# Softmax maxima of every logits block reduced to 32 columns of a table in SBUF, instead of one running maximum in PSUM

## The chip, the cores and the metric

The kernel runs on one core of a Trainium2 chip. The metric is the time on the device of one execution, in microseconds (us); less is better. A core has five engines that run side by side and meet only through semaphores: PE multiplies matrices and writes PSUM, DVE does elementwise work and reductions, ACT evaluates functions and copies, POOL does slower elementwise work on SBUF alone, and SP issues transfers. Each engine runs its own instructions in order.

## The reference

Four cross-attention layers run one after the other on a state of 4 batches x 512 positions x 256 channels, against a context of 4 x 1024 keys x 512 channels. Layers 0, 2 and 3 have 16 heads of width 64 and a bias on at most four keys ("masked" layers below); layer 1 has 16 heads of width 16 with 4 shared key/value heads and an RMS norm ahead of it ("grouped").

```python
q = (x @ Wq) split in heads;  k = (ctx @ Wk);  v = (ctx @ Wv)
logits = einsum('bhqd,bhkd->bhqk', q, k) * scale      # 512 queries x 1024 keys per head
logits += col_bias                                    # layers 0, 2, 3: four key columns
probs = softmax(logits, axis=-1)
x = einsum('bhqk,bhkd->bhqd', probs, v) @ Wo + bo + x # layer 1: without bo
```

The change is in the maximum over the keys that the softmax subtracts.

## The kernel before

A **group** is two heads of one batch in one layer. It has 128 groups: 96 masked and 32 grouped. The logits of a group are laid out with keys on the partitions: block t (of `NT` = 8) holds 128 keys on the partitions and 2 heads x 512 queries = 1024 columns, and lies in `g.st[t]` in SBUF. The maximum that a query needs therefore runs over 8 blocks and over the 128 partitions.

**Order.** Two hand-written strings, `MASKED_TURNS` and `GROUPED_TURNS`, lay the groups out in 96 steps. Each step has one masked group `g`; in 32 of them (steps 12 to 19, 22 to 29, 32 to 39 and 68 to 75) a grouped group `lam`, whose logits were made at the end of the step before, is finished beside it. Below these are the *mixed* steps. All instructions are issued in an order written by hand; the order in the source is the order on each engine's queue. One step does, in this order:

1. POOL: `subtract(lam, t)` (L886), the grouped logits less their maximum, 8 times.
2. `scores(g)` (L803 to L817): for each block, PE makes the logits in two banks of PSUM (L803; for block 0 also the bias, L809), ACT copies them to `g.st[t]` (L813), and from block 1 on DVE does `top = max(top, g.st[t])` (L817), where `top` is the first block's own place in PSUM, `g.mx_place`.
3. `max_quarters(g)` on DVE: `over_quarter` (L854) turns each 32 x 32 square of `top` and reduces it, so that 128 x 1024 becomes 128 x 32 in PSUM; then a fold over the four quarters of the partitions: a copy (L864), a maximum (L865), a copy (L866) and four maxima into `g.every` (L869). In every one of these, one input lies in PSUM. `max_everywhere(g)` (L880) turns the 32 columns back into a 128 x 1024 tile: in PSUM for a masked group, in SBUF for a grouped one.
4. `attend(g1)` on PE (L833): the group of the step before times its values.
5. `subtract(g, t)` on DVE (L888), `exponentials(g, t)` on ACT (L894) and, behind each, the running sum of the exponentials on POOL (L933). Behind them `normalise(g1)` on DVE, whose `reciprocal_sums` uses `over_quarter` again (L854 to L968) and `scale_out` (L979).
6. Meanwhile PE fills its time with projections (L514, L553, L608, L721, L997). In a mixed step, `attend(lam)` comes among them (L833), then `keep_even` (L843) and `keep_odd` (L847).
7. If the next step is mixed, `logits_pair(coming, i)` (L780 to L792) four times: PE makes two blocks, ACT copies them (L786), DVE takes the running maximum (L792); behind the last, `max_quarters` and `max_everywhere` of `coming`.

In 40 of the steps without a grouped group (41 to 64 and 77 to 92), keys or values are made by seven products in place of eight; those have small additions on POOL (L580, L591, L645).

**PSUM** has 8 banks. `Place()` takes two neighbouring banks, the pair that was given back longest ago, and `back()` returns them; all of this is settled when the program is written, and the waits follow from who used the banks last. `g.mx_place` is held from a group's first block until L854 has read it; `max_quarters` holds a further single bank while it folds.

Of the kernel before, what the change touches and what calls it, by code (L numbers as in the profile page):

```python
# [12 lines left out]
ALU = mybir.AluOpType  # L13
AX = mybir.AxisListType
PSUM = bass.MemoryType.PSUM

P = 128
B, S, C = 4, 512, 256
T, CT = 1024, 512
NI = S // P  # L20
NT = T // P
# [59 lines left out]
def kernel(ctx: ExitStack, tc: tile.TileContext, a: dict, out: bass.AP):  # L81
    nc = tc.nc
# [8 lines left out]
    def t_(shape, tag, name, bufs=1, dtype=FP):  # L91
        return sb.tile(shape, dtype, tag=tag, name=name, bufs=bufs)
# [35 lines left out]
    def take_set(g):  # L128
        g.set = sets_free.pop(sets_free.index(min(sets_free)))
        g.st = [st_slot((NT + 1) * g.set + t) for t in range(NT)]  # L130
        g.mx = st_slot((NT + 1) * g.set + NT)
# [643 lines left out]
    def logits_pair(g, i):  # L775
        ws = [Place(), Place()]
        for odd in range(2):
            for j in range(2):
                rows = slice(64 * odd + 32 * j, 64 * odd + 32 * (j + 1))
                nc.tensor.matmul(  # L780
                    ws[odd].ap[:, j * S : (j + 1) * S], lhsT=g.kt[rows, i * P : (i + 1) * P],
                    rhs=g.qt[rows, :], start=True, stop=True,
                )
        for odd, w in enumerate(ws):
            t = 2 * i + odd
            nc.scalar.copy(g.st[t], w.ap)  # L786
            if t == 0:
                g.mx_place = w
            else:
                w.back()  # L790
                top = g.mx_place.ap
                nc.vector.tensor_tensor(top, top, g.st[t], ALU.max)  # L792

    def scores(g):
        take_set(g)
        g.mx_place = Place()
        for t in range(NT):

            w = Place() if t else g.mx_place
            m = w.ap  # L800
            keys = slice(t * P, (t + 1) * P)
            for j in range(2):
                nc.tensor.matmul(  # L803
                    m[:, j * S : (j + 1) * S], lhsT=g.kt[g.rows[j], keys], rhs=g.qt[g.rows[j], :],
                    start=True, stop=t > 0,
                )
            if t == 0:
                for j in range(2):
                    nc.tensor.matmul(  # L809
                        m[:, j * S : (j + 1) * S], lhsT=aug_k[g.l][g.rows[j], keys],  # L810
                        rhs=aug_q[g.rows[j], :], start=False, stop=True,
                    )
            nc.scalar.copy(g.st[t], m)  # L813
            if t:
                w.back()
                top = g.mx_place.ap
                nc.vector.tensor_tensor(top, top, g.st[t], ALU.max)  # L817

    def place_out(g, width=1):
        g.place = Place(width)  # L820
# [29 lines left out]

    def over_quarter(out_, of, op):
        nc.vector.tensor_reduce(  # L854
            out_, of.rearrange("p (b x) -> p b x", x=32), AX.X, op, apply_transpose=True
        )

    def max_quarters(g):
        w = Place(1)
        quarter, half = w.ap[:, 0:32], w.ap[0:64, 32:64]  # L860
        other = t_([64, 32], "other_max", f"other_max_{g.name}")
        over_quarter(quarter, g.mx_place.ap, ALU.max)
        g.mx_place.back()
        nc.vector.tensor_copy(other, quarter[64:128, :])  # L864
        nc.vector.tensor_tensor(half, quarter[0:64, :], other, ALU.max)  # L865
        nc.vector.tensor_copy(other[0:32, :], half[32:64, :])  # L866
        g.every = t_([P, 2 * S // 32, 1], "every", f"every_{g.name}")
        for h in range(4):
            nc.vector.tensor_tensor(  # L869
                g.every[32 * h : 32 * (h + 1), :, 0], half[0:32, :], other[0:32, :], ALU.max  # L870
            )
        w.back()

    def max_everywhere(g):
        if g.masked:
# [76 lines left out]
    def reciprocal_sums(g, m):  # L952

        quarter, half = m[:, 0:32], m[0:64, 32:64]
        other = t_([64, 32], "other", f"other_{g.name}")
        short = t_([P, S // 32, 1], "short", f"short_{g.name}")
        over_quarter(quarter, g.acc, ALU.add)
        nc.vector.tensor_copy(other, quarter[64:128, :])
        nc.vector.tensor_tensor(half, quarter[0:64, :], other, ALU.add)
        nc.vector.tensor_copy(other[0:32, :], half[32:64, :])  # L960
        for h in range(4):
            cols = slice(h // 2 * S // 32, (h // 2 + 1) * S // 32)
            nc.vector.tensor_tensor(
                short[32 * h : 32 * (h + 1), :, 0], half[0:32, cols], other[0:32, cols], ALU.add
            )
        nc.vector.reciprocal(short, short)
        g.ot = t_([P, S], "ot", f"ot_{g.name}", bufs=3)
        nc.vector.transpose(  # L968
            g.ot.rearrange("p (c r) -> p c r", r=32), short.to_broadcast([P, S // 32, 32])
        )  # L970

    def normalise(g):
        w = Place(1)
        reciprocal_sums(g, w.ap)
        w.back()
        scale_out(g)
# [80 lines left out]
    def at(n):  # L1057
        return steps[n] if 0 <= n < len(steps) else (None, None)
# [80 lines left out]
    for n in range(len(steps) + 2):  # L1139
        g, lam = at(n)  # L1140
# [77 lines left out]
        def pair(i):  # L1218
            if i == 0:
                behind_exponentials()  # L1220
                take_set(coming)
            logits_pair(coming, i)
            if i == NT // 2 - 1:
                max_quarters(coming)
                max_everywhere(coming)
# [11 lines left out]
        if g:  # L1237
            g.now = NT if masked_at(g.n + 1) else 4
            scores(g)
# [5 lines left out]
        if g:  # L1245
            max_quarters(g)
            max_everywhere(g)
# [144 lines left out]
```

## Time and profile before

| | before |
|---|---|
| median of 3 runs | 3578.74 us (3578.55 to 3579.28) |
| time of the profiled execution | 3578.93 us |
| its span, first to last instruction | 3577.2 us |
| busy: PE / DVE / POOL / ACT | 98% / 85% / 70% / 66% of the span |
| granted PE clock, mean | 0.995 |

The profile is of one execution. Its span leaves out some 1.7 us around the first and the last instruction. "Busy" counts time in which at least one instruction of the engine is under way; matmuls overlap, and their ends are modelled, so a PE that is 98% busy isn't one that works at its peak for 98% of the time. A group of instructions is named by its line in the kernel. In a chain of waits the text names what released each step.

### The profile page before, as it was taken

The page shows a single profiled execution, that of the slowest core. Times are in us where ns is not written, and L with a number is a line of the kernel's source. Part 1 is how long each engine was busy: PE and PEld are TensorE (multiplying, and loading weights), DVE is VectorE, ACT ScalarE, POOL GpSimd, SP SyncE. Part 2 cuts the span into 40 slices and gives each one's busy share as a digit, 9 for nine tenths or more (in the row PEclk, how much of TensorE's full clock was granted, in tenths as well). Part 3 has the DMA queues.
Part 4 walks back from the last instruction along what each step waited for, and adds up shares of the span by engine and source line. Part 5 has one row for each costly group of instructions (what it writes and reads, how often), then busy time and mean ns, then how long its engine had stood idle before and what let it go on. Part 6 is the DMA issues. An engine that isn't in the chain of part 4 may idle for free.

```text
span 3577.2 us, 42743 instructions
## 1 busy us (share of the span) xinstructions
PE 3495.1 (98%) x15390; PEld 1703.6 (48%) x15390; DVE 3045.3 (85%) x4174; ACT 2352.9 (66%) x2737; POOL 2495.9 (70%) x1273
## 2 busy tenths in 40 slices
PE   8999999999999999999999999999999999999998
PEld 4454444444444444444554545454444445454554
DVE  7878788987889978889888888888788988888887
ACT  4565577775777757777565666665577775666664
POOL 3565477774777747777678778777477776769774
PEclk9999999999999999999999999999999999999999
DMA  3222101002100020001001111010201011002110
GB/s 90 62 93 82 56 20 46 23 19 56 39 23 23 19 78 17 23 23 43 27 27 50 33 33 51 27 51 18 57 22 38 23 34 43 26 27 74 33 32 7
DMA packets 159384, 140.16 MB, mean 39 GB/s; under 512 B 42424, under 2 KB 142264, under 8 KB 158660
## 3 DMA queue, kind: packets, MB, share of 16 engines
q1 hardware_dynamic: 153518, 124.32, 11.2%
q0 software_dynamic: 2560, 8.39, 0.7%
q10 hardware_dynamic: 3094, 4.72, 0.6%
q8 instruction: 122, 2.00, 0.2%
q14 instruction: 90, 0.74, 0.1%
HBM read 122.71 MB, written 10.49 MB: 37 GB/s over the span
## 4 chain that ended last, share of the span: by engine, by line
PE 67%; DVE 23%; ACT 7%; issue 3%; POOL 1%; ACTq 0%; DMA 0%; DVEq 0%; SPq 0%; POOLq 0%
PE ps L608 13%; PE ps L803 13%; PE ps L833 13%; PE ps L514 9%; DVE ps L817 8%; PE ps L553 7%; DVE st L888 5%; ACT st L894 4%; PE ps L780 3%; PE ps L721 3%; PE ps L997 3%; DVE ps L854 2%; DVE ps L880 1%; DVE ps L792 1%; ACT st L786 1%
## 5 line engine op out<-in xcount | busy, mean ns | idle before, releaser
L933 POOL TENSOR_TENSOR st<-st 128x1024 f32<-128x1024 f32 x668 | 1581.0, 2367 | 725.6 <-ACT st L894 680.8
L894 ACT ACTIVATE st<-st 128x1024 f32<-128x1024 f32 x1024 | 1036.3, 1058 | 300.1 <-DVE st L888 233.6
L817 DVE TENSOR_TENSOR ps<-ps,st 128x1024 f32<-128x1024 f32 x672 | 828.0, 1232 | 295.7 <-ACT st L813 234.2
L888 DVE TENSOR_TENSOR st<-st,ps 128x1024 f32<-128x1024 f32 x768 | 883.5, 1216 | 3.3
L886 POOL TENSOR_TENSOR st<-st 128x1024 f32<-128x1024 f32 x256 | 596.8, 2374 | 312.4 <-DVE st L880 207.0
L833 PE MATMUL ps<-st,v 128*64 128x512 f32 (+1 forms) x4064 | 800.7, 595 | 9.0 <-ACT st L894 8.9
L813 ACT COPY st<-ps 128x1024 f32<-128x1024 f32 x768 | 716.6, 1048 | 96.5 <-PE ps L809 65.1
L803 PE MATMUL ps<-qt,kt 64*128 64x512 f32 x3072 | 719.5, 601 | 26.4 <-DVE ps L854 19.6
L833 PEld LDWEIGHTS ps<-st,v 128*64 128x64 f32 (+1 forms) x4064 | 241.4, 130 | 550.2 <-issue 435.5
L803 PEld LDWEIGHTS ps<-qt,kt 64*128 64x128 f32 x3072 | 301.9, 186 | 382.4 <-issue 131.3
L514 PE MATMUL ps<-ctx,wk 128*128 128x512 f32 x896 | 417.1, 611 | 2.2 <-ACT ctx L416 1.1
L553 PE MATMUL ps<-wv,ctx 128*128 128x256 f32 x1792 | 408.0, 382 | 0.0
L553 PEld LDWEIGHTS ps<-wv,ctx 128*128 128x128 f32 x1792 | 335.5, 190 | 102.4 <-issue 59.4
L792 DVE TENSOR_TENSOR ps<-ps,st 128x1024 f32<-128x1024 f32 x224 | 276.1, 1232 | 73.3 <-ACT st L786 60.2
L786 ACT COPY st<-ps 128x1024 f32<-128x1024 f32 x256 | 247.4, 1014 | 83.1 <-PE ps L780 80.2
L514 PEld LDWEIGHTS ps<-ctx,wk 128*128 128x128 f32 x896 | 167.3, 193 | 239.5 <-issue 215.5
L608 PE MATMUL ps<-st 128*128 128x128 f32 (+1 forms) x1200 | 229.0, 339 | 6.4 <-ACT ps L631 6.4
L623 ACT COPY st<-ps 128x512 f32<-128x512 f32 x40 | 23.4, 585 | 301.6 <-PE ps L608 301.6
L780 PE MATMUL ps<-qt,kt 32*128 32x512 f32 x1024 | 183.3, 640 | 18.0 <-DVE o L847 9.7
L608 PEld LDWEIGHTS ps<-st 128*128 128x128 f32 x1200 | 158.6, 192 | 75.1 <-issue 65.1
L721 PE MATMUL ps<-x,wq 128*128 128x512 f32 x384 | 186.2, 608 | 1.3 <-ACT x L379 1.1
L997 PE MATMUL ps<-ot,wo 128*128 128x512 f32 x384 | 175.8, 600 | 0.7 <-DVE ot L979 0.7
(177 smaller groups left out, 2833.1 us busy)
## 6 DMA issues: line engine op xcount, KB each, us to landing
ctx<-kept SPq DMA_DIRECT2D x24, 1024.0 KB
wk<-in_L_xattn_Wk_dram SPq DMA_DIRECT2D x47, 512.0 KB
wv<-in_L_xattn_Wv_dram SPq DMA_DIRECT2D x47, 512.0 KB
wq<-in_L_xattn_Wq_dram SPq DMA_DIRECT2D x96, 128.0 KB
wo<-in_L_xattn_Wo_dram SPq DMA_DIRECT2D x96, 128.0 KB
st<-kept SPq DMA_DIRECT2D x4, 2048.0 KB
kept<-st SPq DMA_DIRECT2D x12, 512.0 KB
qt<-qt ACTq DMA_DIRECT2D x32, 128.0 KB
```

What stands on the lines that cost most here:

```text
L514: nc.tensor.matmul(m, lhsT=g.w["k"][:, k, :], rhs=ctx_half[g.b, n][:, k, :], start=(k == 0), stop=(k == KT - 1),)
L553: nc.tensor.matmul(m[:, half * 2 * P : (half + 1) * 2 * P], lhsT=ctx_half[g.b, t // 4][:, k, t % 4 * P : (t % 4 + 1) * P], rhs=g.w["v2"][: ...
L608: nc.tensor.matmul(m if is_keys else m[:, q], lhsT=right[:, k, :] if is_keys else left_[:, k, q], rhs=left_[:, k, :] if is_keys else right ...
L792: nc.vector.tensor_tensor(top, top, g.st[t], ALU.max)
L803: nc.tensor.matmul(m[:, j * S : (j + 1) * S], lhsT=g.kt[g.rows[j], keys], rhs=g.qt[g.rows[j], :], start=True, stop=t > 0,)
L813: nc.scalar.copy(g.st[t], m)
L817: nc.vector.tensor_tensor(top, top, g.st[t], ALU.max)
L833: nc.tensor.matmul(g.po[at, :], lhsT=g.v[:, t, rows], rhs=g.st[t][:, j * S : (j + 1) * S], start=(t == first), stop=(t == last),)
L886: nc.gpsimd.tensor_tensor(g.st[t], g.st[t], g.mb, ALU.subtract)
L888: nc.vector.tensor_tensor(g.st[t], g.st[t], g.mb, ALU.subtract)
L894: nc.scalar.activation(st, st, AF.Exp)
L933: nc.gpsimd.tensor_tensor(g.acc, g.st[0] if t == 1 else g.acc, g.st[t], ALU.add)
```

## The change

The running maximum goes. Every block, the first included, is given to `over_quarter` by itself as soon as it lies in SBUF, and its 128 x 32 result goes to one eighth of a new table `tops` in SBUF (128 x 8 x 32). After the last block one reduction over the eight takes 128 x 256 to 128 x 32, read in strides of 32 elements. The fold over the quarters is as it was, but its operands now lie in `g.every` and in parts of `tops`, so in SBUF. No place in PSUM is held for a maximum, and `scores` and `logits_pair` give each block's place back when ACT has copied it. `reciprocal_sums` takes part of `tops` as its scratch in place of a tile of its own.

```diff
@@ logits_pair
             t = 2 * i + odd
             nc.scalar.copy(g.st[t], w.ap)
-            if t == 0:
-                g.mx_place = w
-            else:
-                w.back()
-                top = g.mx_place.ap
-                nc.vector.tensor_tensor(top, top, g.st[t], ALU.max)
+            w.back()
+            block_max(g, t)
@@ scores
         take_set(g)
-        g.mx_place = Place()
         for t in range(NT):
-            w = Place() if t else g.mx_place
+            w = Place()
...
             nc.scalar.copy(g.st[t], m)
-            if t:
-                w.back()
-                top = g.mx_place.ap
-                nc.vector.tensor_tensor(top, top, g.st[t], ALU.max)
+            w.back()
+            block_max(g, t)
@@
+    tops = t_([P, NT, 32], "tops", "tops")
...
+    def block_max(g, t):
+        over_quarter(tops[:, t, :], g.st[t], ALU.max)
+
     def max_quarters(g):
-        w = Place(1)
-        quarter, half = w.ap[:, 0:32], w.ap[0:64, 32:64]
-        other = t_([64, 32], "other_max", f"other_max_{g.name}")
-        over_quarter(quarter, g.mx_place.ap, ALU.max)
-        g.mx_place.back()
+        g.every = t_([P, 2 * S // 32, 1], "every", f"every_{g.name}")
+        quarter, half, other = g.every[:, :, 0], tops[0:64, 0, :], tops[0:64, 1, :]
+        nc.vector.tensor_reduce(quarter, tops.rearrange("p t b -> p b t"), AX.X, ALU.max)
         nc.vector.tensor_copy(other, quarter[64:128, :])
         nc.vector.tensor_tensor(half, quarter[0:64, :], other, ALU.max)
         nc.vector.tensor_copy(other[0:32, :], half[32:64, :])
-        g.every = t_([P, 2 * S // 32, 1], "every", f"every_{g.name}")
         for h in range(4):
             nc.vector.tensor_tensor(
                 g.every[32 * h : 32 * (h + 1), :, 0], half[0:32, :], other[0:32, :], ALU.max
             )
-        w.back()
@@ reciprocal_sums
         quarter, half = m[:, 0:32], m[0:64, 32:64]
-        other = t_([64, 32], "other", f"other_{g.name}")
+        other = tops[0:64, 1, :]
```

## The prediction

> **What bounds the kernel now.** I read the page's busy times first, then the steps one by one, then waits and timelines of the steps that looked different.
>
> ```profile
> span 3577.2 us, 42743 instructions
> PE 3495.1 (98%) x15390; PEld 1703.6 (48%) x15390; DVE 3045.3 (85%) x4174; ACT 2352.9 (66%) x2737; POOL 2495.9 (70%) x1273
> PE 67%; DVE 23%; ACT 7%; issue 3%; POOL 1%; ACTq 0%; DMA 0%; DVEq 0%; SPq 0%; POOLq 0%
> ```
>
> PE sets the pace, but a quarter of the chain that ended last lies on DVE. The windows by step say where. Below, columns are the window, its length, then busy time of PE, PEld, DVE, ACT, POOL: two mixed steps, then two steps without a grouped group.
>
> ```profile
> 584.50:634.10 49.60, 47.69 (x180) 18.18 (x178) 45.40 (x66) 35.58 (x40) 35.19 (x15) 1.00 0.20 65
> 634.10:675.50 41.40, 40.67 (x204) 20.96 (x202) 36.52 (x46) 33.57 (x38) 35.72 (x17) 1.00 0.09 22
> 1794.80:1826.40 31.60, 31.60 (x108) 12.80 (x106) 28.76 (x40) 19.24 (x23) 24.68 (x15) 1.00 0.08 24
> 1826.40:1855.20 28.80, 28.80 (x186) 18.68 (x184) 25.08 (x35) 18.73 (x23) 18.99 (x13) 1.00 0.10 31
> ```
>
> The last two are PE without a gap: maxima there have room, since a group's blocks are attended only a step later. In the mixed steps DVE is 45.4 of 49.6 and 36.5 of 41.4 us busy, and what is left is mostly the 0.02 to 0.1 us between its instructions. Its timeline in the first of them (start, length, line, idle before):
>
> ```profile
> 588.25 1.25 DVE L880 STREAM_TRANSPOSE st<-every 128x1024 f32<-128x1024 f32 x1
> 589.41 9.23 DVE L817 TENSOR_TENSOR ps<-ps,st 128x1024 f32<-128x1024 f32 x7
> 598.74 1.26 DVE L854 TRANSPOSE_TENSOR_REDUCE ps<-ps 128x32 f32<-128x1024 f32 x1
> 600.04 0.19 DVE L864 COPY other_max<-ps 64x32 f32<-64x32 f32 x1
> 600.27 0.19 DVE L865 TENSOR_TENSOR ps<-ps,other_max 64x32 f32<-64x32 f32 x1
> 600.49 0.18 DVE L866 COPY other_max<-ps 32x32 f32<-32x32 f32 x1
> 600.71 0.76 DVE L869 TENSOR_TENSOR every<-ps,other_max 32x32 f32<-32x32 f32 x4
> 601.58 1.26 DVE L880 STREAM_TRANSPOSE ps<-every 128x1024 f32<-128x1024 f32 x1
> ...
> 618.66 0.69 DVE L847 TENSOR_TENSOR o<-o,ps 64x512 f32<-64x512 f32 x1 [1.18 <-ACT o L843]
> ...
> 628.80 2.57 DVE L792 TENSOR_TENSOR ps<-ps,st 128x1024 f32<-128x1024 f32 x2 [0.41 <-ACT st L786]
> ```
>
> In 50 us DVE waits for others twice, 1.6 us in all; in the next step (1.0, 1.0, 0.5 and 0.6 us) 3.1. So the change is decided in the 32 mixed steps, where DVE has 4.7 us to spare in a pair of 91. POOL at the same time:
>
> ```profile
> 589.63 18.65 POOL L886 TENSOR_TENSOR st<-st 128x1024 f32<-128x1024 f32 x8 [8.84 <-DVE st L880]
> 608.25 17.04 POOL L933 TENSOR_TENSOR st<-st 128x1024 f32<-128x1024 f32 x7
> ```
>
> The reader is to see that the masked group's fold (600.0 to 601.5) falls into POOL's eight subtractions.
>
> **Removed and added on DVE.** Busy time alone: 896 maxima (672 of L817, 224 of L792) x 1.232 = 1104 us and 128 L854 x 1.265 = 162 us go; 1024 reductions of a block from SBUF x 1.257 (the L854 row ps<-st) = 1287 us come, and 128 reductions of 128 x 256. These aren't in the trace; the nearest, L231, takes 0.304 us for 144 columns, L245 0.253 for 96, so 0.0011 a column and 0.42 for 256. A stride of 32 elements costs nothing in the reciprocals (L744 with it 0.254, L966 without 0.253), so 128 x 0.42 = 54 us. Sum +75 us, and that misleads, because the old maxima are a chain. Seven L817 and the L854 take 10.63 us (589.41 to 600.04), 1.34 from start to start for 1.23 of work: each waits for the one before. Blocks in the table don't depend on each other. Independent instructions overlap: L888 starts each 1.13 for 1.22 of work, and L880 of 1.25 at 588.25 is followed by an independent one after 1.16. Bounds for a reduction's start to start: 1.13 to 1.36 (its 1.26 and the 0.10 of a chain). I take 1.16, the other turning instruction: 7 x 1.16 + 1.36 + 0.46 = 9.94, so 0.7 us less per group (0.9 less to 0.7 more), 2.8 us per pair of mixed steps, which has four groups. The fold itself: the operands from SBUF in place of PSUM, some 0.01 each by L854's two rows (1.265 and 1.257): nothing. `other` in the table is written in DVE's own order, behind the fold that read it: nothing. No transfer and no other queue is moved.
>
> [...]
>
> **PSUM.** The place of the maximum is free sooner, and it has been waited for:
>
> ```profile
>   DVE ps L854: 52.4, 32
> ```
>
> These are waits of L803's weight loads and matmuls for L854, 52.4 us in 32 times, all at the start of mixed steps. With a fourth pair of banks PE goes on there, until ACT's copies (1.05 us each) hold it. Where DVE is the limit the gain isn't added to that of DVE; elsewhere it is nothing, as PE has no gap.
>
> **The fold's inputs.** L865 and the four L869 had one input in PSUM and get two in SBUF; the copies L864 and L866 go from SBUF to SBUF. The trace has no such DVE instruction beside a POOL one, apart from the mask's set-up, where POOL issues gathers:
>
> ```profile
> L283 DVE CAST st<-st x3: 426/481/573, 16.2 to 20.9; 128x512 f32<-128x512 bf16 x3
> ...
> L869 DVE TENSOR_TENSOR every<-ps,other_max x512: 177/181/184, 48.8 to 3546.5; 32x32 f32<-32x32 f32 x171
> ```
>
> The same instruction between SBUF and SBUF takes 426 to 573 ns there, while L869, with an input in PSUM, keeps within 177 to 184 over 512 times, whatever POOL does. So I can't take the new fold to be free of POOL. Bounds: at the lower end 0 more, at the upper each of the seven waits for one POOL instruction (L886, 2372 ns): 16.6 us, cut off where POOL runs dry. It does: 608.3 ends the subtractions, and L933 needs exponentials, which need L888, which stands behind the fold. From 600.0 that is 8.2 us, in the next step (fold at 647.2, POOL to 654.3) 7.1; as the fold comes 0.7 sooner, 8 on average. I take the upper end, since the only row of this sort shows a dependence, and seven waits exceed the cap twice over.
>
> [...]
>
> Behind the waiting fold stand L880, eight L888, L1019, the sums (L854 to L979), L847 and the next grouped group's maxima and L880; ACT's exponentials wait for L888 (233.6 us before), POOL's next subtractions for that L880, PE's grouped attend for both. The masked fold meets L886 in 28 of 32 mixed steps; in the first of each run (12, 22, 32, 68) POOL is done or nearly. Grouped folds run before POOL starts. Elsewhere POOL is idle at the fold or has an L591 of 0.7 us, and PE's bound hides it.
>
> **Sum.** 28 x 8 = 224 us of wait. DVE's spare time takes 14 pairs x (4.7 + 2.8) = 105. The last mixed step of each run is followed by one where DVE is 65% busy, which hides about half of 4 x 8: 16. So +103 us: 3578.9 (profiled; the median is 0.2 lower) + 103 = 3682. Own range: 3638 (7 us, the four last folds hidden whole: 196 - 105 - 32 = +59) to 3760 (reductions at 1.36, so 14 x 5.6 more).
>
> **Rivals.**
> A, faster: the fold doesn't wait. For it: 28 folds beside POOL went undisturbed so far; against it: they read PSUM. Then DVE saves 2.8 us in each of 16 pairs, 45 us: 3534; with a good half of L803's 52 us on top 3500, and at 1.36 nothing, 3579.
> B, near even: copies don't meet POOL and the four L869 pass as one, so 1.2 (half an L886) + 2.4 = 3.6 us: 28 x 3.6 = 101 against 105: 3575, 3550 to 3605.
> C, slower on another ground: the reductions do wait for one another (1.36) and the fold doesn't wait: +2.8 us per pair against 4.7 spare; up to 20 us where the spare time lies wrongly: 3590. It decides if the start to start of block reductions is above 1.30.
>
> **How the numbers follow.** Forecast 0.45, A 0.32, B 0.18, C 0.05. 0.2% (7 us) is what a measurement can tell from none. Faster: 0.30 of A and 0.05 of B; same: 0.02 of A, 0.05 of B, 0.01 of C; slower: the rest, 0.57. The predicted time is the likeliest case's, 3682. The range 3520 to 3750 leaves out the low end of A and the high end of the forecast.
>
> **What would show it.** Right: a fold of 7 to 9 us in place of 1.43 in mixed steps, its instructions starting as an L886 ends; mixed pairs of 97 us and more; other steps unchanged; block reductions 1.16 apart; no wait of L803 for a maximum. Wrong: folds of 1.4 us everywhere (A), 3 to 5 us (B), or reductions 1.3 apart (C).

## The result: 5.9% slower, twice the loss that was forecast

| | before | after |
|---|---|---|
| median | 3579.0 us (4 runs, 3578.6 to 3579.9) | 3790.4 us (4 runs, 3789.0 to 3792.8) |
| ratio, 95% interval | | 1.0592 [1.0578, 1.0605] |
| span of the profiled execution | 3577.2 us | 3787.2 us |
| mean granted PE clock | 0.995 | 0.971 |

The change costs 211 us. The forecast was 103, and the time lies above the whole range. First the page of the changed kernel: span, busy times, the shares of the chain that ended last, and two of the costliest groups (line, engine, shapes, count; then busy us and mean ns of one; then idle time before them).

```profile
span 3787.2 us, 42056 instructions
PE 3548.9 (94%) x15390; PEld 1707.9 (45%) x15390; DVE 3332.3 (88%) x4302; ACT 2358.1 (62%) x2737; POOL 2494.0 (66%) x1273
PE 60%; DVE 29%; ACT 8%; issue 2%; ACTq 0%; POOL 0%; DMA 0%; DVEq 0%; POOLq 0%
L848 DVE TRANSPOSE_TENSOR_REDUCE tops<-st 128x32 f32<-128x1024 f32 x1024 | 1175.3, 1209 | 277.7 <-ACT st L807 241.4
L863 DVE TENSOR_TENSOR every<-tops 32x32 f32<-32x32 f32 x512 | 189.5, 370 | 9.7
```

DVE is 287 us busier, and the chain lies less on PE and more on DVE. What DVE waits for POOL lies in this busy time: it shows in the length of the instructions (the idle time before L863 is 9.7 us in all, as it was before L869). So the engines don't meet through semaphores alone, as the section on the chip has it. The block reductions aren't the reason: 1209 ns against 1232 for the old maximum. But L863, four instructions on 32 x 32 elements (L869 before), takes 370 ns each where it took 180. The same two mixed steps as in the prediction, then the two later steps (window, its length, busy time of PE, PEld, DVE, ACT, POOL, then the granted clock):

```profile
594.40:649.50 55.10, 47.90 (x182) 17.50 (x180) 52.51 (x69) 35.40 (x40) 35.18 (x15) 0.94 0.17 58
649.50:697.50 48.00, 43.69 (x206) 21.35 (x204) 45.19 (x47) 33.61 (x38) 35.65 (x17) 0.93 0.07 20
1915.30:1947.00 31.70, 31.70 (x108) 12.85 (x106) 28.31 (x40) 19.42 (x23) 24.80 (x15) 1.00 0.08 25
1947.00:1975.70 28.70, 28.70 (x184) 18.67 (x182) 26.06 (x37) 19.04 (x23) 18.81 (x12) 1.00 0.10 28
```

These two later steps are unchanged (31.6 and 28.8 before). The mixed pair went from 91.0 to 103.1 us, DVE's busy time in it from 81.9 to 97.7, and the granted clock from 1.00 to 0.94 and 0.93. DVE's timeline in the first of the two mixed steps (start, length), and POOL's beside it:

```profile
607.52 0.60 DVE L858 TENSOR_REDUCE every<-tops 128x32 f32<-128x256 f32 x1
608.15 2.20 DVE L859 COPY tops<-every 64x32 f32<-64x32 f32 x1
610.39 2.28 DVE L860 TENSOR_TENSOR tops<-every,tops 64x32 f32<-64x32 f32 x1
612.71 2.26 DVE L861 COPY tops<-tops 32x32 f32<-32x32 f32 x1
615.00 2.87 DVE L863 TENSOR_TENSOR every<-tops 32x32 f32<-32x32 f32 x4
```

```profile
598.62 18.62 POOL L879 TENSOR_TENSOR st<-st 128x1024 f32<-128x1024 f32 x8 [9.17 <-ACT st L807]
623.55 9.72 POOL L926 TENSOR_TENSOR st<-st 128x1024 f32<-128x1024 f32 x4 [6.31 <-ACT st L887]
```

The masked group's fold lasts until POOL's eight subtractions end, at 617.24: three instructions and the first L863 each take about as long as one subtraction (these are 2.33 us apart) in place of 0.18, and the last three L863 pass at once. The table reduction before them, 0.60 us, isn't held. POOL loses nothing: its 256 subtractions are busy for 595.5 us, 596.8 before. What the late fold does to PE shows in PE's timeline (in brackets: idle before, and what ended it):

```profile
614.67 3.60 PE L514 MATMUL ps<-ctx,wk 128*128 128x512 f32 x8
624.01 5.55 PE L825 MATMUL ps<-st,v 128*32 128x512 f32 x28 [5.74 <-ACT qt L727]
```

Between the fold and PE stand these, on DVE and on ACT:

```profile
619.27 3.48 DVE L881 TENSOR_TENSOR st<-st,ps 128x1024 f32<-128x1024 f32 x3
620.52 2.95 ACT L887 ACTIVATE st<-st 128x1024 f32<-128x1024 f32 x3 [9.12 <-DVE st L881]
623.38 0.57 ACT L727 ACTIVATE qt<-ps 128x512 f32<-128x512 f32 x1
```

The reader is to see the chain: the fold, DVE's subtractions L881, ACT's exponentials L887, and behind the first three of them in ACT's queue the evacuation L727 (a copy out of PSUM), at whose end PE finds a place in PSUM. PE waits 5.7 us, and the 28 matmuls behind the wait take 5.55. Before the change the same 28 (L833 there) came without a wait and took 3.63:

```profile
610.20 3.63 PE L833 MATMUL ps<-st,v 128*32 128x512 f32 x28
```

Waits of this sort, the first two rows below, are most of PE's 238 us of idle time in the whole execution (us in all, times, longest):

```profile
PE ps L825 <- ACT qt L727: 80.2, 13, 7.7
PE ps L825 <- ACT st L887: 66.5, 39, 2.3
PE ps L608 <- ACT ps L631: 40.6, 7, 9.0
```

Before, L833, the same attend, waited for L894, the exponentials, 8.9 us in all. The third row is a place that the prediction left out: seven later steps. In one of them, DVE's fold and then POOL:

```profile
2048.73 2.26 DVE L861 COPY tops<-tops 32x32 f32<-32x32 f32 x1
2051.02 7.05 DVE L863 TENSOR_TENSOR every<-tops 32x32 f32<-32x32 f32 x4
```

```profile
2047.93 0.72 POOL L591 TENSOR_TENSOR st<-wk,st 128x256 f32<-128x256 f32 x1
2048.61 2.35 POOL L580 TENSOR_TENSOR st<-ctx 128x1024 f32<-128x1024 f32 x1
2051.03 2.38 POOL L580 TENSOR_TENSOR st<-st,ctx 128x1024 f32<-128x1024 f32 x1
2053.38 2.35 POOL L580 TENSOR_TENSOR st<-ctx,ctx 128x1024 f32<-128x1024 f32 x1
2055.68 2.34 POOL L580 TENSOR_TENSOR st<-ctx,st 128x1024 f32<-128x1024 f32 x1
```

Four L580 of 2.35 us follow the short L591 there, and the fold waits for each of them: L861 for the first, three of the L863 for the others. The first L863, at 2051.02, starts just ahead of the second L580, at 2051.03, and takes 0.18 us; the same is found in five of the seven steps. That step went from 33.7 to 43.9 us.

### The profile page after: what moved, and what is told of

It reads as the page before. It is cut to its first block, busy times and chain, and to the rows that moved or that the text cites. A ratio compares the mean times of both kernels' runs of the same rounds, so it can differ in the third digit from the quotient of the medians.

```text
span 3787.2 us, 42056 instructions
## 1 busy us (share of the span) xinstructions
PE 3548.9 (94%) x15390; PEld 1707.9 (45%) x15390; DVE 3332.3 (88%) x4302; ACT 2358.1 (62%) x2737; POOL 2494.0 (66%) x1273
## 4 chain that ended last, share of the span: by engine, by line
PE 60%; DVE 29%; ACT 8%; issue 2%; ACTq 0%; POOL 0%; DMA 0%; DVEq 0%; POOLq 0%
PE ps L608 12%; DVE tops L848 11%; PE ps L825 11%; PE ps L797 11%; PE ps L514 8%; PE ps L553 7%; ACT st L887 6%; PE ps L780 4%; DVE every L863 4%; DVE st L881 3%; PE ps L721 3%; DVE tops L861 2%; DVE tops L860 2%; PE ps L990 2%; DVE tops L859 2%
## 5 line engine op out<-in xcount | busy, mean ns | idle before, releaser
L848 DVE TRANSPOSE_TENSOR_REDUCE tops<-st 128x32 f32<-128x1024 f32 x1024 | 1175.3, 1209 | 277.7 <-ACT st L807 241.4
L887 ACT ACTIVATE st<-st 128x1024 f32<-128x1024 f32 x1024 | 1033.5, 1057 | 470.9 <-DVE st L881 389.8
L825 PE MATMUL ps<-st,v 128*64 128x512 f32 (+1 forms) x4064 | 865.1, 636 | 162.4 <-ACT qt L727 80.2
L881 DVE TENSOR_TENSOR st<-st,ps 128x1024 f32<-128x1024 f32 x768 | 883.5, 1216 | 3.3
L879 POOL TENSOR_TENSOR st<-st 128x1024 f32<-128x1024 f32 x256 | 595.5, 2368 | 286.0 <-ACT st L807 171.7
L797 PE MATMUL ps<-qt,kt 64*128 64x512 f32 x3072 | 704.3, 596 | 2.1 <-ACT st L416 0.8
L825 PEld LDWEIGHTS ps<-st,v 128*64 128x64 f32 (+1 forms) x4064 | 248.8, 135 | 751.2 <-issue 459.1
L608 PE MATMUL ps<-st 128*128 128x128 f32 (+1 forms) x1200 | 238.4, 348 | 40.6 <-ACT ps L631 40.6
L863 DVE TENSOR_TENSOR every<-tops 32x32 f32<-32x32 f32 x512 | 189.5, 370 | 9.7
L780 PE MATMUL ps<-qt,kt 32*128 32x512 f32 x1024 | 175.4, 679 | 5.4 <-DVE ot L972 2.6
## 6 DMA issues: line engine op xcount, KB each, us to landing
st<-kept SPq DMA_DIRECT2D x4, 2048.0 KB, 10.3
```

What stands on the lines that cost most here:

```text
L608: nc.tensor.matmul(m if is_keys else m[:, q], lhsT=right[:, k, :] if is_keys else left_[:, k, q], rhs=left_[:, k, :] if is_keys else right ...
L797: nc.tensor.matmul(m[:, j * S : (j + 1) * S], lhsT=g.kt[g.rows[j], keys], rhs=g.qt[g.rows[j], :], start=True, stop=t > 0,)
L825: nc.tensor.matmul(g.po[at, :], lhsT=g.v[:, t, rows], rhs=g.st[t][:, j * S : (j + 1) * S], start=(t == first), stop=(t == last),)
L848: nc.vector.tensor_reduce(out_, of.rearrange("p (b x) -> p b x", x=32), AX.X, op, apply_transpose=True)
L863: nc.vector.tensor_tensor(g.every[32 * h : 32 * (h + 1), :, 0], half[0:32, :], other[0:32, :], ALU.max)
L879: nc.gpsimd.tensor_tensor(g.st[t], g.st[t], g.mb, ALU.subtract)
```

## The experiments

Each line number is that of the kernel it is about. Times are medians; a "before" beside them was measured on the same chip.

### Is the fold's place the whole of it?

**e1_psum_fold**: the changed kernel, but quarter and half lie in PSUM, as before.

```diff
-        quarter, half, other = g.every[:, :, 0], tops[0:64, 0, :], tops[0:64, 1, :]
+        w = Place(1)
+        quarter, half, other = w.ap[:, 0:32], w.ap[0:64, 32:64], tops[0:64, 1, :]
...
+        w.back()
```

> The changed kernel with the fold alone taken back to PSUM (quarter and half in one bank, other in SBUF); block reductions, table and PSUM places as changed. Theory P (a DVE instruction whose operands all lie in SBUF waits for the POOL instruction under way): folds of 2.0 us in all 128 groups, the granted clock back to 0.99 or more, and a time under that of before, 3500 us (3480 to 3535): about 80 us off, 4 to 5 us for each odd mixed step and 1 for each even one, since L848 starts 1.13 apart instead of 1.34 and L797 no longer waits for a place. Rival Q (the loss comes from the block reductions, the strided reduction of 0.60 us or the new order of PSUM places): over 3700 us, since all of these are kept.

**e2_old_max_sbuf_fold**: the kernel before, running maximum and all, with only the fold's operands moved to SBUF.

```diff
-        w = Place(1)
-        quarter, half = w.ap[:, 0:32], w.ap[0:64, 32:64]
-        other = t_([64, 32], "other_max", f"other_max_{g.name}")
+        g.every = t_([P, 2 * S // 32, 1], "every", f"every_{g.name}")
+        scratch = t_([64, 2, 32], "other_max", f"other_max_{g.name}")
+        quarter, half, other = g.every[:, :, 0], scratch[:, 0, :], scratch[:, 1, :]
...
-        g.every = t_([P, 2 * S // 32, 1], "every", f"every_{g.name}")
...
-        w.back()
```

> The kernel before with the fold alone moved to SBUF (running maximum in PSUM kept). Theory P: folds of 9 to 10 us beside L886 in 28 mixed steps and of 3 to 11 us beside L580 and L591 in the later steps; about 3800 us (3770 to 3860), granted clock near 0.97, and more than the changed kernel, as the shorter chain and the freed places are missing. Rival Q: 3579 us, folds of 1.4 us.

Measured: the first 3518.0 us (5 runs; before 3580.0; ratio 0.9828 [0.9814, 0.9841], clock 0.996), the second 3855.3 (4 runs; 1.0769 [1.0752, 1.0785], clock 0.969). The fold's place alone is worth 272 us in the changed kernel and 275 in the old one; the rest of the change, without it, is a gain of 62. In the first, DVE's timeline of the same step, POOL's, and the two steps' windows:

```profile
587.04 3.46 DVE L848 TRANSPOSE_TENSOR_REDUCE tops<-st 128x32 f32<-128x1024 f32 x3
590.60 0.60 DVE L859 TENSOR_REDUCE ps<-tops 128x32 f32<-128x256 f32 x1
591.23 0.19 DVE L860 COPY tops<-ps 64x32 f32<-64x32 f32 x1
591.46 0.19 DVE L861 TENSOR_TENSOR ps<-ps,tops 64x32 f32<-64x32 f32 x1
591.69 0.18 DVE L862 COPY tops<-ps 32x32 f32<-32x32 f32 x1
591.90 0.77 DVE L864 TENSOR_TENSOR every<-ps,tops 32x32 f32<-32x32 f32 x4
592.77 1.26 DVE L875 STREAM_TRANSPOSE ps<-every 128x1024 f32<-128x1024 f32 x1
```

```profile
581.63 18.69 POOL L881 TENSOR_TENSOR st<-st 128x1024 f32<-128x1024 f32 x8 [7.36 <-DVE st L875]
```

```profile
577.30:624.30 47.00, 46.99 (x182) 17.45 (x180) 44.29 (x68) 35.39 (x40) 35.25 (x15) 1.00 0.21 69
624.30:664.70 40.40, 40.40 (x206) 20.79 (x204) 37.41 (x47) 33.46 (x38) 35.77 (x17) 1.00 0.08 22
```

POOL is in the middle of its eight, and the fold takes 1.4 us all the same: one operand in PSUM was enough here. In this kernel PE has no gap left in the pair (87.39 of 87.40 us), while DVE has 5.7.

### Which instructions wait?

To the kernel with the fold in PSUM one unused instruction between parts of the table is added behind the table reduction: **e3_one_copy** a copy, **e4_one_max** a maximum of two inputs.

```diff
+        nc.vector.tensor_copy(tops[0:64, 2, :], tops[0:64, 3, :])
```

> The first kernel of this call with one more DVE instruction between the reduction of the table and the fold: a copy of 64 x 32 from SBUF to SBUF whose result nothing uses. Theory P: it takes 0.17 us where POOL is idle and up to 2.3 us, until the end of the running L879, in the mixed steps; the rest of the fold keeps its 1.4 us; time at most 15 us over the first kernel, as DVE has that much to spare. Theory P2 (only instructions with two inputs in SBUF wait, copies do not): 0.17 us everywhere.

```diff
+        nc.vector.tensor_tensor(tops[0:64, 2, :], tops[0:64, 3, :], tops[0:64, 4, :], ALU.max)
```

> As the run ahead of it, but the further instruction is a maximum of two 64 x 32 inputs, both in SBUF, into SBUF. Theories P and P2 alike: 0.18 us where POOL is idle, up to 2.3 us in the mixed steps. Theory P3 (only copies wait): 0.18 us everywhere.

One run each: 3567.4 and 3567.6 us, some 49 more than without and not the 15 at most that were expected. The added line in each (ns: least, median, most):

```profile
L860 DVE COPY tops<-tops x128: 173/174/2417, 46.0 to 3533.5; 64x32 f32<-64x32 f32 x128
```

```profile
L860 DVE TENSOR_TENSOR tops<-tops x128: 182/184/2393, 46.2 to 3533.7; 64x32 f32<-64x32 f32 x128
```

Both wait, by up to one whole POOL instruction (2.24 and 2.21 us over the median, where a subtraction takes 2.33), so the theories by which only one kind does fall. The waits of the added instruction come to 63 us in e3_one_copy and 61 in e4_one_max, 54 and 53 of it in mixed steps; one such instruction in each group is enough for 49 us.

### Is it the lateness, and does spare time hide it?

**e5_plain_delay** and **e10_delay_three**: the kernel with the fold in PSUM; behind the fold of 28 mixed steps, seven (three) block reductions are done again into an unused part of the table. They read one input, and nothing of them waits for POOL: the 1220 of e5_plain_delay take 1196 to 1248 ns, the 1024 of the changed kernel 1196 to 1247.

```diff
+            if lam and lam.u:
+                for t in range(7):
+                    over_quarter(tops[:, 2, :], g.st[t], ALU.max)
             max_everywhere(g)
```

> The kernel with the fold in PSUM, and in the same 28 mixed steps seven further block reductions (single input, result unused) behind the masked group's fold: 7 x 1.13 = 7.9 us in which DVE works and waits for nobody. Theory P (what costs is that DVE is late by that much; the spare time of DVE in the mixed steps hides little of it): 28 x 7.9 = 221 us less some 10%, so +200 on 3518: 3718 (3690 to 3740), with the granted clock near 0.975 as in the changed kernel, and the later steps as fast as before. Rival S (the meeting with POOL costs something beyond the lateness of DVE, on POOL too): at most +130, under 3650, clock near 0.99.

> As the run with seven further block reductions (3758), with three: 3 x 1.13 = 3.4 us of lateness in each of 28 mixed steps, 95 us in all. If lateness costs in proportion, as from 3518 to 3758 for 221 us: 3518 + 103 = 3621 (3600 to 3635). If there were 4.7 us of spare time per pair of steps that hides the first part, as the prediction had it: 3518 + 95 - 66 = 3547.

Measured 3757.7 us (4 runs; 1.0501 [1.0485, 1.0517], clock 0.976) and 3618.5 (4 runs; 1.0105 [1.0089, 1.0120], clock 0.988). DVE's timelines, seven and then three:

```profile
609.22 0.77 DVE L864 TENSOR_TENSOR every<-ps,tops 32x32 f32<-32x32 f32 x4
610.02 8.93 DVE L848 TRANSPOSE_TENSOR_REDUCE tops<-st 128x32 f32<-128x1024 f32 x7
618.87 1.22 DVE L875 STREAM_TRANSPOSE ps<-every 128x1024 f32<-128x1024 f32 x1
```

```profile
601.35 0.76 DVE L864 TENSOR_TENSOR every<-ps,tops 32x32 f32<-32x32 f32 x4
602.14 3.81 DVE L848 TRANSPOSE_TENSOR_REDUCE tops<-st 128x32 f32<-128x1024 f32 x3
605.87 1.22 DVE L875 STREAM_TRANSPOSE ps<-every 128x1024 f32<-128x1024 f32 x1
```

The reductions write one place, so they start 1.28 us apart and not 1.13, and the delay is larger than the expectations counted: from the fold's end to L875 8.88 and 3.76 us, 0.10 without them, so 8.78 and 3.66 more. Times 28 that is 246 and 102 us; the time rose by 240 and 100.5, 0.98 of it both times (the four runs of e10 lie between 3612.3 and 3623.0 us, so there it is 0.92 to 1.02). So the lateness of the fold alone is enough for a loss of this size, and the smaller delay isn't hidden any better than the larger one: had the 4.7 us of idle time that the prediction counted on in each pair hidden their part, 66 of the 102 us would be missing.

PE shows how, by its attend L825 (busy us, mean ns | idle before). In order: the fold in PSUM with three and with seven reductions, then the changed kernel.

```profile
L825 PE MATMUL ps<-st,v 128*64 128x512 f32 (+1 forms) x4064 | 823.3, 598 | 50.5 <-ACT st L889 46.8 <-ACT qt L727 2.0 <-ACT qt L731 1.7
```

```profile
L825 PE MATMUL ps<-st,v 128*64 128x512 f32 (+1 forms) x4064 | 870.4, 634 | 152.7 <-ACT st L889 74.3 <-ACT qt L727 67.2 <-ACT qt L731 11.1
```

```profile
L825 PE MATMUL ps<-st,v 128*64 128x512 f32 (+1 forms) x4064 | 865.1, 636 | 162.4 <-ACT qt L727 80.2 <-ACT st L887 66.5 <-ACT qt L731 15.6
```

Without a delay the same 4064 matmuls are busy for 800.3 us with 0.2 us of idle time before them. Seven reductions bring 152.5 us of idle time, 94 less than the 246 of lateness: so much PE still had to do. But L825 itself then takes 70 us longer, and that returns most of what was hidden. Three bring 50 and 23. Over all PE work the count is full: against the fold in PSUM, PE is 152 us more idle and 88 longer busy with seven, 64 and 41 with three, 196 and 76 in the changed kernel.

### Where do the 272 us lie?

**e6_mixed_only**: the fold in SBUF in mixed steps alone.

```diff
+        w = None if beside else Place(1)
+        quarter, half, other = (
+            (g.every[:, :, 0], tops[0:64, 0, :], tops[0:64, 1, :]) if beside
+            else (w.ap[:, 0:32], w.ap[0:64, 32:64], tops[0:64, 1, :])
+        )
...
+        if w:
+            w.back()
...
-            max_quarters(g)
+            max_quarters(g, lam)
```

> The fold in SBUF in the 32 mixed steps' masked groups alone, in PSUM everywhere else. Theory P: the mixed steps' share of the loss, 210 us by the steps of the two traces: 3728 (3710 to 3745); the seven steps 41, 47, 55, 63, 77, 85 and 87, where L580 and L591 run on POOL, are back to their 32 to 34 us, which leaves 60 us between this run and the changed kernel. If the later steps were late for another reason: within 15 us of 3790.

3735.3 us (4 runs; 1.0437 [1.0421, 1.0453], clock 0.977). So of the 272 us between the two places of the fold, 217 lie in mixed steps and 55 elsewhere, which the trace puts in the seven later steps with the four L580.

### How much is the clock? (inconclusive)

**e7_warm**: the changed kernel with 24 small unused matmuls before the grouped attend, meant to fill PE's idle time.

```diff
+                warm = Place(1)
+                for _ in range(24):
+                    nc.tensor.matmul(warm.ap, lhsT=aug_k[0], rhs=aug_q, start=True, stop=True)
+                warm.back()
                 attend(lam)
```

> The changed kernel with 24 further matmuls (128 x 512 bf16, about 0.21 us each at the full clock, result unused) ahead of the grouped attend of each mixed step, where PE sits idle for some 6 us in odd steps. Theory T (part of the loss is the clock that PE is granted after such an idle stretch): granted clock 0.985 or more in place of 0.971, half-clock time well under the changed kernel's 222 us, and 20 to 60 us less than 3790 although PE has 5 us more to do per step. Rival U (the lower clock lies in stretches where PE waits anyway): 3790 or more, up to 3870 where the added work isn't hidden in the even steps.

3849.5 us (4 runs; 1.0753 [1.0737, 1.0770], clock 0.978). PE's timeline says why it settles nothing:

```profile
629.32 0.59 PE L1301 MATMUL ps<-aug_q,aug_k 128*128 128x512 bf16 x1 [5.66 <-DVE x L1012]
630.13 5.89 PE L1301 MATMUL ps<-aug_q,aug_k 128*128 128x512 bf16 x22 [0.22 <-issue]
635.95 3.64 PE L825 MATMUL ps<-st,v 128*32 128x512 f32 x32
```

The time lies where the rival had it, but that decides nothing: the added matmuls need a place in PSUM too, so they wait 5.66 us themselves, and stand behind the gap rather than in it. (The 0.21 us that the expectation counts for one is what L809 shows in the kernel before, on 512 bf16 columns: the next matmul starts 0.21 us after it.) One thing fits the clock: 32 attend matmuls behind the added ones take 3.64 us in this step, where 28 right behind the gap took 5.55 (32 without a gap, in e1_psum_fold, 4.68). The slow one of the three is the one that stands right behind a gap.

### What are the gain's 62 us?

**e9_place_held**: the fold in PSUM, but block 0 stays in its PSUM place until the last block and is reduced from there, so that the place comes free as late as before.

```diff
-            w.back()
-            block_max(g, t)
+            if t == 0:
+                g.mx_place = w
+            else:
+                w.back()
+                block_max(g, t)
@@ max_quarters
+        over_quarter(tops[:, 0, :], g.mx_place.ap, ALU.max)
+        g.mx_place.back()
```

> The kernel with the fold in PSUM, but block 0 is reduced from its place in PSUM, behind the last block, and the place is given back only then, as before the change; the other seven blocks and the table as changed. It gives back the late release of one pair of banks and keeps the unchained reductions. If the gain of the fold in PSUM (3580 to 3518) came from DVE's shorter chain alone: 3518 to 3525. If it came from the freed place: about 3570 and waits of L797 for the reduction of about 50 us as before. I expect both in part, 3540 (3525 to 3560).

3555.1 us (5 runs; before 3579.8; 0.9933 [0.9919, 0.9946]). The score matmuls L800 wait for a place again, as they did before (us, times):

```profile
  DVE tops L854: 39.1, 32
```

So 37 of the 62 us go with block 0 and its place, and 25 are left for reductions that don't wait for one another. How much of the 37 is the place alone this run doesn't show, since the edit also has block 0 reduced last, as the kernel before did. A grouped group's blocks come from ACT with gaps, so a reduction left for the end can't use them: in 31 of the 32 grouped groups the fold starts 1.3 to 1.9 us later behind DVE's work before the first block than with the fold in PSUM alone, 43 us in all.

**e8_table_turned**: the fold in PSUM, and the table laid out so that the eight maxima of a column lie together; the blocks are written with a stride, and the table is read without one.

```diff
-    tops = t_([P, NT, 32], "tops", "tops")
+    tops = t_([P, 32, NT], "tops", "tops")
...
-        over_quarter(tops[:, t, :], g.st[t], ALU.max)
+        over_quarter(tops[:, :, t], g.st[t], ALU.max)
...
+        nc.vector.tensor_reduce(quarter, tops, AX.X, ALU.max)
...
```

> The kernel with the fold in PSUM, the table laid out 32 x 8 in place of 8 x 32: block reductions write in strides of 8 elements, the reduction of the table reads without a stride. If the stride is what makes that reduction 0.60 us in place of the 0.42 worked out from L231: 0.42 us, 0.2 us less in each of 128 groups, of which those in mixed steps count: 64 x 0.2 = 13 us at most, so 3505 to 3518. If the 0.60 is the number of outputs or else: 3518. If the strided writes cost: block reductions over 1.20 us, and over 3518.

3507.1 us (5 runs; before 3578.9; 0.9802 [0.9789, 0.9816]), the fastest of all, 2.0% below the kernel before. The table reduction, with the stride in the read and then without:

```profile
L859 DVE TENSOR_REDUCE ps<-tops x128: 597/609/639, 45.7 to 3482.7; 128x32 f32<-128x256 f32 x128
```

```profile
L859 DVE TENSOR_REDUCE ps<-tops x128: 427/428/430, 45.9 to 3472.8; 128x32 f32<-128x256 f32 x128
```

## Why the prediction was wrong in size

**Right: the wait itself.** The forecast had 28 folds wait 8 us, 224. From the table reduction to the last L863 the fold takes 10.3 us in the first step of a mixed pair and 9.8 on average in the second (9.2 to 10.1), against 2.03 undisturbed: 16 x 8.3 + 12 x 7.8 = 226. It was cut off where POOL's subtractions end, as argued, and it was right not to read the smooth L869 row as safety: e1, e3 and e4 show that what protected it was its input in PSUM (L861 of e1 takes 191 to 192 ns in all 128 groups, the added instructions of e3 and e4 up to 2417 and 2393). But the row that it took the upper end from, three casts of 426 to 573 ns, differs by 0.15 us, and the waits were some 2 us each; that the upper end was the case no row of before showed, and so far the size was luck.

**Wrong, the step that failed:** "DVE's spare time takes 14 pairs x (4.7 + 2.8) = 105", and with it the 16 us that the last step of each run "hides about half of". Of 226 us of waiting (235 with 2.2 in each of the four first steps) e6 finds 217 in the time, so that 18 us were hidden and not the 66 + 16 = 82 of the forecast. The 2.8 was a real saving; the 4.7 was idle time of DVE elsewhere in the pair, summed as if a late fold could draw on it. What stands behind the fold is not DVE's next work but PE, by way of L881, the exponentials and the evacuation in ACT's queue, and PE is full: with the fold in PSUM 87.39 of 87.40 us. The first microseconds do vanish, since PE has work until the attend, but the attend that comes after the gap is then slower (L825 in all by 70 us in e5, by 23 in e10), so that 0.98 of an added delay came through, small or large (e10, e5).

**Wrong: a term set to nothing.** "Elsewhere POOL is idle at the fold or has an L591 of 0.7 us, and PE's bound hides it." In seven later steps the L591 were only the first of POOL's queue, with L580 behind them; their folds took up to 11.4 us, and cost 55.

**Not foreseen: PE's clock.** L825 is busy for 65 us more in the changed kernel than with its fold in PSUM, at the same median of 592 ns a matmul but a longest of 1063 against 643. All PE work is 75.7 us longer (3548.9 against 3473.2), and the granted clock is 0.971 against 0.996. An estimate from these clocks and spans: if PE had had work all the time, the clock would account for at most 0.029 x 3787 - 0.004 x 3515 = 96 us. How much of the 272 would go if the clock held wasn't settled. In the first of the two mixed steps PE is idle from 618.27 to 624.01 us, and the granted clock is 1.00 from 607 to 621, 0.51 on average from 621 to 628 and 1.00 again from 628 to 631: the slow attend (5.55 us in place of 3.63, from 624.01 on) falls for the most part into the stretch at the lower clock. Whether the idle time brings the lower clock, and how much of it does, no run here tests.

**Mis-sized: the gain.** Rival A, in which the fold doesn't wait, was put at 3534; e1 is this case, and is 3518. Block reductions start 1.13 apart (three take 3.46 us, of which the last 1.20), not 1.16. What the prediction didn't add, the freed place in PSUM and block 0 reduced first, brought 37 us; L803's 52.4 us of waits left room for the place to bring it, but its own share isn't shown. Against it the table reduction takes 0.60 us and not 0.42: "a stride of 32 elements costs nothing" held for 16 columns of a reciprocal and not here; without the stride it is 0.43 (e8).

**The sum with what was measured:** 3579 - 62 + 217 + 55 = 3789, against 3790. These terms are differences between the runs, so their sum parts the time and doesn't test it; e2 does, where the fold's place is worth 275 us in the old kernel too. From the forecast's 103: 11 for more waiting (235 for 224), 64 for what wasn't hidden (18 for 82), 55 for the later steps, less 23 for the gain (62 for 14 x 2.8 = 39), which is 210. Rival C falls with the 1.13. Rival B, copies free and four L863 passing as one, falls with e3, and in the timeline: both copies wait.

**What the wait showed.** In the first of the two mixed steps, copies and two-input instructions with all their operands in SBUF took 2.20 to 2.28 us, on 64 x 32 and on 32 x 32 elements, in place of the 0.18 to 0.19 of e1. The price was paid for each of four instructions anew, and POOL's busy time didn't rise by it (595.5 us against 596.8 for its 256 subtractions).

## What to carry to other kernels

While POOL worked through SBUF instructions of 2.3 to 2.4 us, a tiny DVE copy or two-input instruction with all its operands in SBUF took up to 2.2 to 2.3 us, in place of 0.17 to 0.19, each time that it found one under way; one input in PSUM avoided it here (0.18 to 0.19 us in e1). Reductions with one input in SBUF weren't held (L858 590 to 635 ns, L848 at most 1247). A wait is not to be set against the idle time of the engine that waits: follow who stands behind it to the engine that is full, and take the wait as lost there unless the trace shows what that engine would do meanwhile. For each place where a step runs, read the other engine's whole queue, not the one instruction under way.

## What the hardware showed that was not expected

- With POOL busy back to back, DVE's next instruction found POOL's next one already under way, four times running (L860 started at 610.39, the subtraction beside it at 610.24), and waited for its end. Once POOL's eight had ended (617.24), the last three L863 passed by 617.87. Where DVE's instruction started first, if only by 0.01 us (L863 at 2051.02, L580 at 2051.03), it took 0.18 us.
- DVE instructions that turn and reduce overlapped where they wrote different places (L848 of e1: 1.13 us from start to start for 1.20 of work) and didn't where they wrote one (the added ones of e5: 1.28).
- Reading 256 numbers a partition at a stride of 32 took 0.61 us (e1) against 0.43 without (e8); writing 32 of them at a stride of eight cost nothing (block reductions take 1.20 us in both).
